# A two-layer transformer block on one core: the order of merging, of the last output projection and of the last tile's mean

## The chip, the core and the metric

The kernel runs on one core of a Trainium2 chip. The metric is the device time of one execution in microseconds. A profile of one execution shows every instruction of the engines: PE (TensorE; PEld is its weight load), DVE (VectorE), ACT (ScalarE), POOL (GpSimd) and SP (SyncE, which issues DMAs).

## What is computed

The input x has 4 x 256 tokens of 512 numbers. Two layers follow, each an attention and a feed-forward step, each added to its input and normalised (mean and variance over the 512 numbers of a token):

```python
x = _layernorm(x + _L0_attn_ref(x, ...))
x = _layernorm(x + _L0_ffn_ref(x, ...))
x = _layernorm(x + _L1_attn_ref(x, w_qkv, w_o))
x = _layernorm(x + _L1_ffn_ref(x, kernel))
```

Layer 1's attention has 8 groups (kv = 0 to 7) of 4 heads of 128 numbers, which share keys and values, with a distance bias and a causal mask. Its output projection is `out @ w_o`, summed over all 8 groups. Its feed-forward step multiplies with a matrix whose 512 rows repeat one block of 64 rows 8 times. All arithmetic is in fp32.

## The kernel before, in words

The tokens stand in 8 tiles of 128 tokens (tt = 0 to 7), two for each batch entry b. `x2[tt]` holds a tile's sum on its way through layer 1. Layer 1's attention is a loop over 64 steps (kv, b, qt), each of 128 queries of 4 heads. `begin1` (L964) makes the scores on PE, adds the bias and takes the maxima on DVE, and makes exponentials and their sums on ACT; `divided` (L282) takes the reciprocals of the sums on DVE (L283) and multiplies the probabilities by them on POOL (L286). `transpose1`, one step later, transposes the probabilities: for kv below 7 by 32x32 blocks on DVE (L312) and DMAs, for kv = 7 on PE (L301). `end1`, one step later again, multiplies with the values on PE (L1012).

For kv below 7, the output projection of both tiles of one b is done with seven products instead of eight (a Strassen scheme in Winograd's form). `outputs1` (L917) first makes four left sums on POOL (`left_sums`, L616 to L621, tile `so`, one buffer); `output_products` then queues the products on PE (L885): four (`po4`), one and five (`po15`, whose second half has the first left sum as weights), six and seven (`po67`, second and third sum), two and three (`po23`, whose second half has the fourth sum). Their results are added on DVE into `x2` (L947, L952) and into `kept[b]` (L898), which collects partial sums over all kv. When the products of b for kv = 6 have been queued, b is put on `merges`; `merge` (L902) then adds `kept[b]` into `x2[2b]` and `x2[2b+1]` with eight additions of 128 x 256 on POOL (L907). The merges 0 to 2 are called from `outputs1` of the next b or from `end1` of kv = 7, merge 3 from `end1`.

For kv = 7, `output1` (L842) multiplies one tile's attention output with the group's weights (four matmuls, L846) and adds it to `x2[tt]` on DVE (L849): the residual. Then `tail1` (L775) of that tile is put on the list of tails. It is a generator; each `yield` ends a piece. Its first piece adds the halves of `x2` on POOL (`half`, L784), takes mean and variance on DVE (`statistics`, L768, tiles `bn_c` and `mv_c`), four times the mean (`four`, L787), `eps` (L789), and the folded and centred tile `xs` (L791). The second transposes `xs` on PE (`pt_xs`, L796) and copies it on ACT (`xsT`, L105). The third multiplies with the feed-forward block on PE (`pf1`, L801), adds on DVE (`z`, L803), takes statistics again (`bn_d`, `mv_d`), forms the reciprocal root on DVE and POOL (`rs`, L808, L809) and the output: on ACT for tiles 0 to 6 (`shift` L820, `yo` L821), on DVE in two halves for tile 7 (L814), each followed by its DMA.

The order of the instructions on each engine is chosen when the program is built: instructions are handed over in the order in which the Python code calls them, and a scheduler may let an instruction pass others. Two calls bind it. `tc.keep_in_program_order` fixes an instruction's place among its engine's, and `tc.issue_after(x)` hands instructions over no earlier than behind the instruction x. [...] After the 64 steps a loop empties the lists `outputs` and `tails` (L1070).

A step or block is named below as (kv, b, qt) or by its b; "pr" tiles are probabilities.

## Time and profile before

| what | value |
|---|---|
| times of three runs, us | 948.67, 951.85, 1353.63 (median 951.85) |
| time of the profiled execution, us | 951.23 |
| its span, first to last instruction, us | 949.3 |
| mean granted TensorE clock | 0.995 of full speed |
| PE busy share of the span | 96% |
| DVE, POOL, ACT busy share | 66%, 47%, 35% |
| the chain that ended last | PE 70%, DVE 12%, POOL 9%, ACT 5% |
| first output product of kv = 6 / start of the last matmul, us from the span's start | 827.93 / 941.83 |

In the rows of a timeline, the first number is the start in us from the span's start, the second the length; then follow engine, line, operation, what is written and read, and in brackets how long the engine sat idle before it and what ended that. Rows of the same kind that follow each other directly are shown as one, with their number behind the x.

### The profile page before, as it was taken

Reading aid. Unit: us, or ns where it says so; the run is one execution under the profiler, and the core shown is the slowest. Engines: PE = TensorE matmul, PEld = TensorE weight load, DVE = VectorE, ACT = ScalarE, POOL = GpSimd, SP = SyncE. Lnnn points to the kernel's source line nnn. Section 1 sums busy time; section 2 is a strip of 40 time slices with the busy share of each in tenths; the row PEclk is TensorE's granted clock in tenths of the full one; section 3 lists DMA queues with packets and bytes.
Section 4 is the critical chain, followed back from the end, with each engine's and each line's share of the span. In section 5 each row is a group of like instructions: output and inputs, shape, how many; then the busy total and the mean of one; then the engine's idle time right before and its main releaser. Section 6 shows DMA issues by size and latency. Waiting matters only on the chain.

```text
span 949.3 us, 11860 instructions
## 1 busy us (share of the span) xinstructions
PE 906.8 (96%) x3849; PEld 554.4 (58%) x3849; DVE 623.8 (66%) x1269; ACT 333.9 (35%) x1216; POOL 444.7 (47%) x462
## 2 busy tenths in 40 slices
PE   7998999898899999999999999999999999999996
PEld 5755555554444445666666566666666666667652
DVE  3986978879434448555676776666666666666566
ACT  2775675677410003323222222122221121214441
POOL 2554553645356124426434533643553534656732
PEclk9999999999999999999999999999999999999998
DMA  9500000000020103543443443353353333432001
GB/s 246 185 1 1 1 2 1 1 1 1 1 89 22 45 1 89 152 111 115 114 130 79 134 132 100 110 140 88 117 139 95 122 89 105 129 89 70 1 34 55
DMA packets 76419, 74.46 MB, mean 78 GB/s; under 512 B 5957, under 2 KB 52678, under 8 KB 76358
## 3 DMA queue, kind: packets, MB, share of 16 engines
q1 hardware_dynamic: 75014, 72.02, 26.4%
q10 hardware_dynamic: 1344, 1.70, 0.6%
q8 instruction: 30, 0.49, 0.2%
q14 instruction: 31, 0.25, 0.1%
HBM read 49.58 MB, written 24.12 MB: 78 GB/s over the span
## 4 chain that ended last, share of the span: by engine, by line
PE 70%; DVE 12%; POOL 9%; ACT 5%; DMA 2%; issue 1%; ACTq 0%; POOLq 0%; SPq 0%; DVEq 0%
PE p_q L636 19%; PE po L885 14%; PE sc L972 7%; PE o L1012 7%; PE p_k L636 5%; PE p_v L636 5%; ACT pr L278 4%; PE py L442 3%; DVE pr L489 3%; PE pf L459 2%; DVE nm L495 2%; PE py L846 2%; POOL x L907 2%; POOL pr L286 2%; DVE prT L103 1%
## 5 line engine op out<-in xcount | busy, mean ns | idle before, releaser
L286 POOL TENSOR_TENSOR pr<-pr,sums 128x512 f32<-128x512 f32 (+1 forms) x128 | 189.5, 1481 | 232.9 <-DVE sums L283 227.4
L278 ACT ACTIVATE pr<-sc,nm 128x128 f32<-128x128 f32 (+1 forms) x256 | 105.0, 419 | 291.1 <-DVE nm L988 277.1
L278 ACT ACTIVATE pr<-pr,nm 128x128 f32<-128x128 f32 (+1 forms) x256 | 113.2, 444 | 39.3 <-DVE sums L283 30.2
L980 DVE SCALAR_TENSOR_TENSOR sc<-table,sc 128x128 f32<-128x128 f32 (+1 forms) x256 | 86.0, 356 | 34.7 <-PE sc L972 32.4
L972 PEld LDWEIGHTS sc<-kT,qT 128*128 128x128 f32 x512 | 82.3, 191 | 35.1 <-issue 29.7
L972 PE MATMUL sc<-kT,qT 128*128 128x256 f32 (+1 forms) x512 | 95.0, 327 | 0.0
L1012 PE MATMUL o<-prT,v 128*128 128x512 f32 x192 | 92.9, 592 | 0.0
L312 DVE STREAM_TRANSPOSE blocks<-pr 128x512 f32<-128x512 f32 x84 | 57.6, 698 | 45.2 <-POOL pr L286 45.1
L650 DVE TENSOR_TENSOR qT<-p_q,qT 128x512 f32<-128x512 f32 x96 | 64.6, 686 | 33.6 <-PE p_q L636 32.8
L988 DVE TENSOR_REDUCE nm<-sc 128x2 f32<-128x512 f32 (+1 forms) x128 | 70.0, 550 | 1.5
L489 DVE TENSOR_TENSOR pr<-sc,causal 128x512 f32<-128x512 f32 (+1 forms) x64 | 60.5, 945 | 10.2 <-PE sc L486 10.0
L301 PE MATMUL pt<-ident,pr 128*128 128x128 f32 x432 | 59.9, 276 | 7.2 <-DVE prT L103 2.1
L495 DVE TENSOR_REDUCE nm<-pr 128x4 f32<-128x512 f32 (+1 forms) x64 | 60.7, 948 | 1.2
L301 PEld LDWEIGHTS pt<-ident,pr 128*128 128x128 f32 x432 | 48.6, 141 | 21.2 <-issue 10.1
L105 ACT COPY o<-o 128x512 f32<-128x512 f32 x29 | 17.0, 587 | 124.9 <-PE o L1012 124.9
L885 PE MATMUL po<-wo,so 128*128 128x256 f32 x224 | 58.0, 381 | 2.1 <-POOL so L616 2.1
L636 PE MATMUL p_q<-x2T,ws_q 128*128 128x512 f32 x128 | 59.8, 592 | 0.0
L636 PE MATMUL p_q<-xt,ws_q 128*128 128x512 f32 x128 | 57.7, 592 | 0.0
L885 PE MATMUL po<-wo,o 128*128 128x256 f32 x224 | 57.7, 380 | 0.0
L636 PE MATMUL p_q<-x2T,wq 128*128 128x512 f32 x128 | 57.6, 592 | 0.0
L105 ACT COPY prT<-pt 128x512 f32<-128x512 f32 x76 | 42.6, 582 | 39.5 <-PE pt L301 39.5
L885 PE MATMUL po<-to,so 128*128 128x256 f32 x224 | 53.3, 381 | 1.0 <-POOL so L619 1.0
(159 smaller groups left out, 1516.8 us busy)
## 6 DMA issues: line engine op xcount, KB each, us to landing
way<-blocks SPq DMA_DIRECT2D x112, 128.0 KB, 2.5
prT<-way SPq DMA_DIRECT2D x28, 512.0 KB, 3.7
wq<-in_L_attn_w_qkv_dram SPq DMA_DIRECT2D x8, 1024.0 KB, 5.1
wo<-in_L_attn_w_o_dram SPq DMA_DIRECT2D x8, 1024.0 KB, 5.4
way<-blocks SPq DMA_DIRECT2D x112, 64.0 KB, 1.8
prT<-way SPq DMA_DIRECT2D x28, 256.0 KB, 2.6
wk<-in_L_attn_w_qkv_dram SPq DMA_DIRECT2D x4, 512.0 KB, 3.8
wv<-in_L_attn_w_qkv_dram SPq DMA_DIRECT2D x2, 1024.0 KB, 6.2
```

What stands on the lines that cost most here:

```text
L278: nc.scalar.activation(pr[:, i, 0:w], sc, AF.Exp, bias=nm[:, i : i + 1], accum_out=sums[:, i : i + 1])
L286: nc.gpsimd.tensor_tensor(pr[:, :, 0:w], pr[:, :, 0:w], sums.unsqueeze(2).to_broadcast([P, G, w]), ALU.mult)
L301: nc.tensor.transpose(pt[:, i, :], pr[:, i, ts(kt, P)], ident)
L489: nc.vector.tensor_tensor(pr[:, :, 0:w], sc[:, :, 0:w], causal[:, 2 * P - w :].unsqueeze(1).to_broadcast([P, G, w]), ALU.add,)
L495: nc.vector.tensor_reduce(nm, pr[:, :, 0:w], AX.X, ALU.max, negate=True)
L636: nc.tensor.matmul(bank, fixed, moving, start=(c == 0), stop=(c == 1))
L650: add = lambda dst, a, b: nc.vector.tensor_tensor(dst, a, b, ALU.add)
L885: nc.tensor.matmul(bank[:, ts(n, HALF)], left[:, c, :], right[:, c, :], start=(c == 0), stop=(c == 1),)
L972: nc.tensor.matmul(sc[:, m, 0:w], qT[:, 2 * j + m, b * S + qt * P : b * S + (qt + 1) * P], kT[:, b * S : b * S + w], start=True, stop=True,)
L980: nc.vector.scalar_tensor_tensor(sc[:, m, 0:w], table[:, 2 * P - w :], slopes[kv * G + 2 * j + m], sc[:, m, 0:w], ALU.mult, ALU.add,)
L988: nc.vector.tensor_reduce(nm[:, 2 * j : 2 * j + 2], sc[:, :, 0:w], AX.X, ALU.max, negate=True)
L1012: nc.tensor.matmul(o, v1[:, 2 * b + kt, ts(kv, P)], prT[:, kt].rearrange("p j h q -> p h j q"), start=(kt == 0), stop=(kt == qt),)
```

## The change

There are three edits.

`divided` returns its POOL instruction, and `begin1` keeps the newest one. `outputs1` binds a merge to that instruction instead of to the last of its own block's left sums. In the compiled program POOL's list changes in one stretch: merge 0 stands ahead of the left sums of b = 1 instead of behind them, merge 1 ahead of those of b = 2, and merge 2 ahead of the division of (7, 1, 0) and of the left sums of b = 3. In merges 0 and 1 the eight additions also stand in another order.

`output1` of tile 7 yields after its second matmul, and the closing loop calls `outputs` ahead of `tails`. In the compiled program PE's list changes in one place: two of tile 7's four output matmuls stand ahead of `pf1_5` instead of behind it.

For tile 7, the residual is a `tensor_tensor_reduce` on DVE, which also sums its result over the row. It is built as two instructions, the main one and one that writes out the sum; the signal to others hangs on the second. `four` is formed from this sum, `xs` follows, and `mv_c` and `eps` come behind `xs`; in the compiled list `bn_c` still stands ahead of `xs`. The lists of ACT and SP are the same as before.

```diff
-        nc.gpsimd.tensor_tensor(
+        return nc.gpsimd.tensor_tensor(
             pr[:, :, 0:w], pr[:, :, 0:w], sums.unsqueeze(2).to_broadcast([P, G, w]), ALU.mult
         )
...
-    def tail1(tt):
+    def tail1(tt, total=None):
...
-        mv = statistics(x, f"c{tt}")
         four = t1.tile([P, 1], F32, tag="four", name=f"four_{tt}", bufs=4)
-        nc.vector.tensor_scalar(four, mv[:, 0:1], 4.0, None, ALU.mult)
+        xs = t1.tile([P, P], F32, tag="xs", name=f"xs_{tt}")
+        add_up = lambda: nc.vector.scalar_tensor_tensor(
+            xs, half[:, 0:P], four, half[:, P:], ALU.subtract, ALU.add
+        )
+        if total is None:
+            mv = statistics(x, f"c{tt}")
+            nc.vector.tensor_scalar(four, mv[:, 0:1], 4.0, None, ALU.mult)
+        else:
+            nc.vector.tensor_scalar(four, total, 4.0 / D, None, ALU.mult)
+            tc.keep_in_program_order(add_up())
+            mv = statistics(x, f"c{tt}")
         eps = t1.tile([P, 1], F32, tag="eps", name=f"eps_{tt}", bufs=4)
         nc.vector.tensor_scalar(eps, mv[:, 1:2], EPS, EPS, ALU.add, ALU.mult)
-        xs = t1.tile([P, P], F32, tag="xs", name=f"xs_{tt}")
-        nc.vector.scalar_tensor_tensor(
-            xs, half[:, 0:P], four, half[:, P:], ALU.subtract, ALU.add
-        )
+        if total is None:
+            add_up()
         yield True
...
-        nc.vector.tensor_tensor(x2[tt], py, x2[tt], ALU.add)
-        tails.append(tail1(tt))
+            if i == 1 and tt == NTT - 1:
+                yield True
+        total = None
+        if tt == NTT - 1:
+            total = t1.tile([P, 1], F32, name="total", bufs=1)
+            nc.vector.tensor_tensor_reduce(
+                out=x2[tt], in0=py, in1=x2[tt], scale=1.0, scalar=0.0,
+                op0=ALU.add, op1=ALU.add, accum_out=total,
+            )
+        else:
+            nc.vector.tensor_tensor(x2[tt], py, x2[tt], ALU.add)
+        tails.append(tail1(tt, total))
         yield True
...
-            done = left_sums(S, A)
+            left_sums(S, A)
             if merges:
-                with tc.issue_after(done.ins):
+                with tc.issue_after(open1["division"].ins):
                     merge()
...
-        divided(pr, sums, w)
+        open1["division"] = divided(pr, sums, w)
         return pr
...
-    while outputs or tails:
-        advance_all(tails, True)
+    while outputs:
         advance(outputs)
         ending.append(True)
+        advance_all(tails, True)
+    while tails:
         advance_all(tails, True)
```

## The prediction, made before the changed kernel ran

> **What bounds the kernel now.** I read the page first (busy time, chain), then the chain in its last 90 us, then the timelines of POOL and PE there, then all engines in the last 20 us.

> ```profile
> PE 906.8 (96%) x3849; PEld 554.4 (58%) x3849; DVE 623.8 (66%) x1269; ACT 333.9 (35%) x1216; POOL 444.7 (47%) x462
> ```

> PE is busy 96% of the span, so a part of the change is worth what it adds to or takes from PE's gaps, plus what it shortens after PE's last product. The chain from 859 to 893 us runs nearly wholly through POOL: POOL's late results make PE's gaps there. POOL's rows (start, length, idle before and its releaser):

> ```profile
> 839.60 1.90 POOL L286 TENSOR_TENSOR pr<-pr,sums 128x1024 f32<-128x1024 f32 x1 [7.16 <-DVE sums L283]
> 843.78 0.73 POOL L616 TENSOR_TENSOR so<-o 128x256 f32<-128x256 f32 x1 [2.29 <-ACT o L105]
> ...
> 846.64 0.72 POOL L907 TENSOR_TENSOR x<-x,kept 128x256 f32<-128x256 f32 x1
> ...
> 852.38 1.04 POOL L286 TENSOR_TENSOR pr<-pr,sums 128x512 f32<-128x512 f32 x1
> 859.34 1.89 POOL L286 TENSOR_TENSOR pr<-pr,sums 128x1024 f32<-128x1024 f32 x1 [5.92 <-DVE sums L283]
> 861.19 0.72 POOL L616 TENSOR_TENSOR so<-o 128x256 f32<-128x256 f32 x1
> ...
> 864.06 0.72 POOL L907 TENSOR_TENSOR x<-x,kept 128x256 f32<-128x256 f32 x1
> ...
> 869.77 2.90 POOL L286 TENSOR_TENSOR pr<-pr,sums 128x512 f32<-128x512 f32 x2
> 875.14 1.04 POOL L286 TENSOR_TENSOR pr<-pr,sums 128x512 f32<-128x512 f32 x1 [2.48 <-DVE sums L283]
> 876.14 0.73 POOL L616 TENSOR_TENSOR so<-o 128x256 f32<-128x256 f32 x1
> ```

> Each merge is eight additions: 846.64 to 852.38, 5.7 us. A group of left sums is four: 861.19 to 864.06, 2.9; its first ends after 0.72. A division takes 1.85 (wide) or 1.0. PE's rows with waits:

> ```profile
> 861.97 1.13 PE L885 MATMUL po<-wo,so 128*128 128x256 f32 x4
> ...
> 870.87 0.65 PE L301 MATMUL pt<-ident,pr 128*128 128x128 f32 x4 [1.73 <-POOL pr L286]
> 871.36 1.06 PE L972 MATMUL sc<-kT,qT 128*128 128x128 f32 x8
> 872.72 0.88 PE L301 MATMUL pt<-ident,pr 128*128 128x128 f32 x6 [0.30 <-POOL pr L286]
> ...
> 877.96 1.03 PE L885 MATMUL po<-wo,so 128*128 128x256 f32 x4
> ...
> 894.68 0.30 PE L796 MATMUL pt_xs<-ident,xs 128*128 128x128 f32 x1 [0.57 <-DVE xs L791]
> ```

> The reader should see that the row at 861.97 starts 0.06 after the sum it needs (861.91): there is no slack for later sums. The end:

> ```profile
> 933.99 1.12 PE L801 MATMUL pf<-wf,xsT 128*128 128x512 f32 x2 [0.88 <-ACT xsT L105]
> 938.70 0.69 DVE L849 TENSOR_TENSOR x<-py,x 128x512 f32<-128x512 f32 x1 [1.58 <-PE py L846]
> 940.62 0.35 DVE L791 SCALAR_TENSOR_TENSOR xs<-half,four 128x128 f32<-128x128 f32 x1
> 943.00 0.75 DVE L803 SCALAR_TENSOR_TENSOR z<-x,mv_c,pf 128x512 f32<-128x512 f32 x1 [0.22 <-PE pf L801]
> ```

> PE's last gap (pt_xs at 932.83 could have been followed at 932.94) is 1.05 us; from 938.66 on, everything is the last tile's chain.

> [...]the division at 852.38 had its sums at 846.46 and stood 5.9 us behind the merge. [...]ScalarE's accumulator reads take 0.19 to 0.21 and end about 0.1 after their main instruction. [...]the trace has 686 for x<-py,x.

> **Part 1, merging.** The compiled order moves merges 0 and 1 from behind to ahead of the left sums of blocks 1 and 2 of kv 6, and merge 2 to ahead of division (7,1,0) and the left sums of block 3. No addition is added or removed and no DMA moves. What stands behind a merge is thereby 5.7 us later on POOL; I follow it in before's clock.

> Merge 0 can start at 841.5, in POOL's idle 2.3 us (the additions PE needs for it end on DVE by 842.6, before the pieces that read them), ends 847.2; sums 847.2 to 850.1, the first at 847.9; PE loads it as weight at 848.7. It just fits, 0.8 to spare. Division (6,3,0) then starts 850.1, 2.3 early. DVE idled 2.8 for it (transpose at 853.45), so its queue moves up as a whole: block transpose 851.1, copy, score additions 852.3 (scores from PE at 851.6 and 852.5), maxima done 855.7; ACT's four exponentials last 1.0, to 856.7; the kept addition ahead of the reciprocal, behind a product ending 855.96, ends 856.7 too. Reciprocal 856.9, division (6,3,1) at 857.0 instead of 859.34.

> Merge 1 follows: 858.9 to 864.6. Block 2's first sum ends 865.3; PE wants it at 861.97: **a new wait of 3.4 us**, with PE's whole queue behind it: the products of block 2, o of (6,3,0), the scores of (7,0,1) and so their softmax on DVE and ACT. DVE's kept addition of this product stands ahead of the reciprocal of (7,0,0), which is thus 867.2, still ahead of POOL's turn for it (867.5). PE is then ready for (7,0,0)'s transposes at 868.97+3.4 = 872.4, and that division is done at 864.6+2.9+1.0 = 868.5, so before's wait until 870.87 is gone: net +1.5. The scores of (7,0,1) come 3.4 later; their sums are ready at about 872.4, the division lasts 872.5 to 874.35, PE goes on at 874.4 instead of 872.72: +1.7.

> Merge 2: 874.35 to 880.1. Then division (7,1,0) to 881.1 and block 3's first sum at 881.8. PE would want it at 877.96+1.7 = 879.66 and gets it at 881.84: +3.9. From there kept 3 waits on POOL for block 3's product (886.1, DVE until 887.0), division (7,1,1) follows at 887.8 to 889.6, ahead of its transposes on PE (890.49+3.9), then the rest of merge 3 and division (7,2,0) to 895.1. The residual of tile 0 follows PE (890.69+3.9, to 895.3), half ends 896.05, xs 896.9, and PE arrives at 894.11+3.9 = 898.0, so the 0.57 wait goes: **+3.3** into the tails, where PE paces all the rest.

> **Part 2, last output projection.** Two matmuls (four passes, 1.72 us) of tile 7 move ahead of pf1_5 into the 1.05 us gap. Their input oT was copied by 929.33. py of tile 7 ends 937.5 instead of 938.66 (932.94 + 1.72 + pf1_5 0.86 + pt_xs 0.11 + 1.72 = 937.35, and 0.16 to drain). Its price: pf1_5 runs 934.66 to 935.7, 0.6 later, so on DVE z_5 starts 935.7 instead of 935.23 and rs_5, last ahead of the residual and 1.89 after z_5's start, ends 937.6. The residual starts 937.6 instead of 938.70, -1.1. If DVE were slower there, the residual would be late next, not PE.

> **Part 3, mean from the residual.** Main instruction: between 0.69[...] and 1.38 (half rate); accumulator read 0.1 to 0.2 more, ahead of any signal to POOL. I take 0.69 and 0.1. POOL's half starts behind shift_5 at 938.6, ends 939.33; bn_c of 0.68 runs meanwhile; xs starts 939.4 instead of 940.62. From xs, the transpose, ACT's copy and pf1_7 take 2.38 to z_7, as before (940.62 to 943.00): 941.8. DVE's own queue needs as long now: mv_c and eps (0.3) stand behind xs, then z_6 to rs_6 (940.90 to 942.78, 1.9). The cover that before was 0.22 of DVE idleness is used up; any more on DVE would count. z_7 is 1.2 earlier than 943.00, and the rest of the chain (6.3 us to the end, the two DMAs in it) is as before. At half rate the residual's signal is 0.7 later and half with it, so 0.6. **-1.2**, bounds -0.5 and -1.3.

> Sum: +3.3 - 1.2 = +2.1 on the profiled 951.23 (span 949.3, 1.9 around it): **953.3**. The two near runs shown, 948.67 and 951.85 (the median, which the profiled run misses by 0.6), say one number wanders by 3 us, more than this effect; about 2%, 19 us, is what a measurement of this kernel can tell from no change.

> **Rivals.** (a) Merging earlier costs PE nothing: its idle 2.3 us on POOL is used, the three POOL waits of PE (1.73+0.30+0.57) go, and the end gains 1.2: 951.23-3.8 = 947.4. For it: POOL is on the chain. Against: the sum at 861.19 starts immediately behind the division, and now has a merge ahead. It decides only if PE reaches the product at 861.97 over 3.4 us later than I have it. (b) Slower: division (6,3,1) is not earlier. Then block 2's first sum comes at 867.6, PE waits 5.7, reaches (7,0,0)'s transposes 3.8 late, and block 3's sums make it about 6: 951.23+6-1.2 = 956. It decides if DVE's queue (kept addition, exponentials) holds the sums until 859. (c) The end gains nothing: the accumulating instruction takes over 2 us. 951.23+3.3 = 954.5. Slower than 2% would need it to take about 18 us more[...], so I leave it 2 in 100.

> **Chances.** Likeliest 0.62 (own range 951.5 to 954.8, terms' bounds alone), (a) 0.13, (b) 0.12, (c) 0.11, the far tail 0.02. The range of 949.3 to 956.5 leaves out most of (a) and the tail, and takes in (b), (c) and the wander. Faster by over 2% 0.01, within 0.97, slower 0.02.

> **What would show it.** Right: PE's po<-wo,so near 862 waits about 3.4 for POOL's L616, the one near 878 about 2.2; the division at 859.34 starts near 857; PE's wait at 870.87 is gone; pf1_5 has no wait behind it, the residual begins 1.1 nearer to its tile's predecessor, xs 1.8 after it. Wrong: no PE wait on left sums, or an accumulating row over 1.4 us.

## The result, and the profile after

| kernel | median, us | lowest to highest | runs | ratio to before [95% interval] |
|---|---|---|---|---|
| before | 949.93 | 947.29 to 1353.63 | 22 | |
| changed | 954.19 | 951.18 to 958.87 | 22 | 1.0046 [1.0033, 1.0059] |

(The 1353.63 is a disturbed execution and is left out of the comparison.) The change makes the kernel slower by 0.46%, some 4.3 us (3.1 to 5.6 by the interval), less than the 2% that count as a difference here, but beyond the interval. The forecast said +2.1. The profiled execution of the changed kernel took 956.8 us, with a span of 954.9 us and a mean TensorE clock of 0.990 (before: 951.23, 949.3, 0.995). First the busy time, from the page of the changed kernel:

```profile
PE 909.2 (95%) x3849; PEld 555.2 (58%) x3849; DVE 624.7 (65%) x1270; ACT 335.3 (35%) x1216; POOL 444.7 (47%) x462
```

POOL's work is the same 444.7 us: the additions were only moved. PE did the same 3849 matmuls, but was busy 2.4 us longer (909.2 against 906.8). That is a first hint that more than waits was added, since idle time is not counted as busy. PE's timeline around the moved merges:

```profile
865.67 1.13 PE L902 MATMUL po<-wo,so 128*128 128x256 f32 x4 [3.50 <-POOL so L616]
866.64 1.68 PE L1029 MATMUL o<-prT,v 128*128 128x512 f32 x2
868.11 2.97 PE L989 MATMUL sc<-kT,qT 128*128 128x256 f32 x8
...
874.37 0.60 PE L301 MATMUL pt<-ident,pr 128*128 128x128 f32 x4
...
876.50 0.88 PE L301 MATMUL pt<-ident,pr 128*128 128x128 f32 x6 [0.64 <-POOL pr L286]
...
883.89 2.06 PE L902 MATMUL po<-wo,so 128*128 128x256 f32 x4 [1.99 <-POOL so L616]
885.75 1.82 PE L1029 MATMUL o<-prT,v 128*128 128x512 f32 x2
```

Both forecast waits are there, 3.50 us for block 2's first left sum and 1.99 for block 3's, and the wait of 1.73 ahead of (7,0,0)'s transposes is gone. But look at the second column: `o<-prT,v x2` takes 1.68 and 1.82 where it takes 1.02 elsewhere, the scores `x8` 2.97 instead of 1.89, and `po<-wo,so x4` 2.06 instead of 1.03. The same matmuls run at about half speed behind each wait. The view by stretches of time says why; its columns are the stretch, its length, the busy time of PE, PEld, DVE, ACT and POOL, and then the granted TensorE clock:

```profile
862.00:865.60 3.60, 0.17 (x1) 0.00 (x0) 0.35 (x2) 1.20 (x7) 3.44 (x6) 1.00 0.55 115
865.60:867.00 1.40, 1.33 (x5) 1.06 (x6) 0.16 (x1) 0.00 (x0) 1.38 (x3) 0.95 0.82 281
867.00:870.40 3.40, 3.40 (x8) 2.19 (x7) 0.96 (x3) 0.59 (x1) 1.73 (x2) 0.52 0.12 42
870.40:880.00 9.60, 8.96 (x48) 7.14 (x47) 5.96 (x16) 5.00 (x19) 5.37 (x7) 1.00 0.00 0
882.00:883.80 1.80, 0.00 (x0) 0.00 (x0) 0.10 (x1) 1.02 (x4) 1.80 (x4) 1.00 0.00 0
883.80:887.40 3.60, 3.51 (x6) 2.16 (x7) 0.69 (x1) 0.00 (x0) 2.76 (x5) 0.53 0.00 0
```

PE idles, resumes, and for about 3.4 us gets a clock of 0.52 or 0.53; then it is 1.00 again (the row from 870.40; behind 887.40 too). Below, this is called a clock fall; its exact edges stand in the section on after_again1 and after_again2. POOL's order came out as worked out: merge 0 begins at 841.54, block 1's sums at 847.38, division (6,3,0) at 850.24 (forecast: 841.5, 847.2, 850.1). The end, on DVE:

```profile
944.52 0.69 DVE L861 CUSTOM_DVE_ANT_0 x<-py,x 128x512 f32<-128x512 f32 x1
945.14 0.08 DVE L861 DVE_READ_ACCUMULATOR2_ANT total<- 128x1 f32 x1
946.29 0.35 DVE L787 SCALAR_TENSOR_TENSOR xs<-half,four 128x128 f32<-128x128 f32 x1 [0.28 <-POOL half L784]
...
948.67 0.75 DVE L810 SCALAR_TENSOR_TENSOR z<-x,mv_c,pf 128x512 f32<-128x512 f32 x1
```

The accumulating residual takes 0.69 us, as the plain one did; its read 0.08. `xs` starts 1.77 us behind it (before: 1.92).

### One clock for all executions

The times from the span's start are not comparable between executions: the division (6,2,1), which stands at 839.60 in the profile of before and ahead of everything that the change moves, starts at 835.29 to 840.11 in the fourteen profiles of this study, although every instruction up to it is in the same order. So this table counts from that division. Rows are named by the experiments below. "First sum" and "fourth sum" are PE's products with these left sums. The end of the span is taken to the hundredth, where the pages round it to a tenth.

| execution | division at | block 2, first sum | block 2, fourth sum | block 3, first sum | pt_xs of tile 0 | residual of tile 7 | its z | end of span | length of last pf1 |
|---|---|---|---|---|---|---|---|---|---|
| before | 839.60 | 22.37 | 28.51 | 38.36 | 55.08 | 99.10 | 103.40 | 109.66 | 1.13 |
| changed | 839.69 | 25.98 | 33.81 | 44.20 | 61.98 | 104.83 | 108.98 | 115.24 | 1.12 |
| after_again1 | 837.75 | 25.95 | 33.78 | 44.15 | 60.24 | 103.08 | 107.22 | 113.49 | 1.13 |
| after_again2 | 840.11 | 25.94 | 33.77 | 44.14 | 60.23 | 103.07 | 107.21 | 113.47 | 1.13 |
| merge_only | 839.73 | 25.97 | 33.74 | 44.13 | 60.21 | 104.21 | 109.06 | 115.33 | 1.67 |
| ends_only | 837.32 | 22.35 | 28.49 | 38.36 | 55.07 | 97.94 | 102.32 | 108.58 | 1.35 |
| projection_only | 837.21 | 22.35 | 28.49 | 38.34 | 55.06 | 97.94 | 103.16 | 109.44 | 2.05 |
| mean_only | 837.53 | 22.35 | 28.49 | 38.35 | 55.06 | 99.08 | 103.00 | 109.27 | 1.12 |
| first_merge_ends | 839.09 | 22.31 | 28.35 | 37.34 | 54.07 | 96.94 | 101.19 | 107.46 | 1.24 |
| two_merges_ends | 837.15 | 25.97 | 33.80 | 42.03 | 58.63 | 101.50 | 106.10 | 112.37 | 1.58 |
| split_second_merge | 837.99 | 22.31 | 28.35 | 36.57 | 53.46 | 96.34 | 100.47 | 106.74 | 1.13 |
| fill_second | 837.45 | 25.97 | 33.81 | 44.20 | 60.28 | 103.13 | 107.27 | 113.55 | 1.13 |
| fill_first_wait | 835.29 | 26.01 | 32.15 | 41.52 | 59.34 | 102.19 | 106.33 | 112.59 | 1.13 |
| fill_first_again | 839.39 | 25.96 | 32.10 | 41.46 | 62.30 | 105.13 | 109.32 | 115.59 | 1.18 |

Up to pt_xs of tile 0 the rows with the same POOL order agree within 0.1 us, except where a clock fall stands between. That makes differences of 0.3 us readable in a single profile that the medians, with intervals of 1.2 us to each side and more, can't give.

### The profile page after: what moved, and what is told of

It is laid out like the page before. It is cut to its first block, busy times and chain, and to the rows that moved or that the text cites. A ratio compares the mean times of both kernels' runs of the same rounds, so it can differ in the third digit from the quotient of the medians.

```text
span 954.9 us, 11860 instructions
## 1 busy us (share of the span) xinstructions
PE 909.2 (95%) x3849; PEld 555.2 (58%) x3849; DVE 624.7 (65%) x1270; ACT 335.3 (35%) x1216; POOL 444.7 (47%) x462
## 4 chain that ended last, share of the span: by engine, by line
PE 73%; DVE 12%; POOL 8%; ACT 5%; issue 1%; DMA 1%; ACTq 0%; POOLq 0%; DVEq 0%
PE p_q L636 19%; PE po L902 15%; PE sc L989 8%; PE o L1029 8%; PE p_k L636 5%; PE p_v L636 5%; ACT pr L278 4%; PE py L442 3%; DVE pr L489 3%; PE pf L459 2%; PE py L853 2%; DVE nm L495 2%; POOL pr L286 2%; PE pq L403 1%; DVE prT L103 1%; POOL x L924 1%
## 5 line engine op out<-in xcount | busy, mean ns | idle before, releaser
L286 POOL TENSOR_TENSOR pr<-pr,sums 128x512 f32<-128x512 f32 (+1 forms) x128 | 189.5, 1481 | 235.1 <-DVE sums L283 224.0
L997 DVE SCALAR_TENSOR_TENSOR sc<-table,sc 128x128 f32<-128x128 f32 (+1 forms) x256 | 86.2, 356 | 37.0 <-PE sc L989 34.7
L301 PE MATMUL pt<-ident,pr 128*128 128x128 f32 x432 | 59.8, 276 | 5.9 <-DVE prT L103 2.1
L105 ACT COPY o<-o 128x512 f32<-128x512 f32 x29 | 17.0, 587 | 132.0 <-PE o L1029 132.0
L301 PEld LDWEIGHTS pt<-ident,pr 128*128 128x128 f32 x432 | 48.6, 141 | 19.6 <-issue 10.2
L105 ACT COPY prT<-pt 128x512 f32<-128x512 f32 x76 | 42.7, 582 | 39.9 <-PE pt L301 39.9
```

The costliest lines, as they stand in the source:

```text
L286: return nc.gpsimd.tensor_tensor(pr[:, :, 0:w], pr[:, :, 0:w], sums.unsqueeze(2).to_broadcast([P, G, w]), ALU.mult)
L301: nc.tensor.transpose(pt[:, i, :], pr[:, i, ts(kt, P)], ident)
L997: nc.vector.scalar_tensor_tensor(sc[:, m, 0:w], table[:, 2 * P - w :], slopes[kv * G + 2 * j + m], sc[:, m, 0:w], ALU.mult, ALU.add,)
```

## The experiments

The theory after this first profile: merging earlier makes two waits on PE, each costs its idle time less the waits that it replaces, and on top of that up to 1.9 us for a clock fall behind it (an estimate: the longer rows above add 1.74 us behind the first wait and 1.83 behind the second). The rivals: the whole loss is idle time on POOL's account, and the long rows belong to the order of instructions; or the end does not gain what was said.

### merge_only and ends_only: the parts alone

The first edit alone (`divided` returns its instruction, `outputs1` binds the merge to it), and the second and third alone (`outputs1` as before).

> Only the merges are moved (part 1); the end is as before. My theory (the loss is PE's two waits for left sums, about 3.4 and 2.0 us, and a halved TensorE clock for some us behind each of them in about half of the executions): PE reaches the first transpose of a tail (pt_xs of tile 0) 3.3 us late without and up to 7 us late with the lower clock, the median is 5 to 6 us above before, ratio 1.005 to 1.007. Rival (the loss lies in the two edits at the end, the accumulating residual above all): ratio 1.000, no late PE at pt_xs.

Measured: 956.45 us median (953.52 to 960.42, 6 runs), ratio 1.0082 [1.0057, 1.0106].

> Only the two edits at the end (parts 2 and 3); the merges stand as before. My theory: 1.3 us shorter than before, ratio 0.9986; z of the last tile starts 1.3 us earlier than 943.0, and no wait of PE for left sums is longer than before's. Rival (the end edits lose): ratio 1.002 or more, z of the last tile later than 943.

Measured: 948.03 us (946.47 to 951.22, 22 runs), ratio 0.9987 [0.9974, 1.0001].

The loss is merging's, the end gains. In the table, merging delays pt_xs of tile 0 by 60.21 - 55.08 = 5.1 us with one clock fall (behind the first wait; the second wait, 2.00 us, had none). The end's edits shorten the end by 109.66 - 108.58 = 1.08 us, and by 0.22 more if the last product had its old length (last column: 1.35 against 1.13). Their median's interval holds 1.000, so the timed runs alone do not show that gain; the anchored trace does, step by step.

### projection_only and mean_only: the end taken apart

On the kernel before, only the second edit:

```diff
+            if i == 1 and tt == NTT - 1:
+                yield True
...
-    while outputs or tails:
-        advance_all(tails, True)
+    while outputs:
         advance(outputs)
         ending.append(True)
+        advance_all(tails, True)
+    while tails:
         advance_all(tails, True)
```

> Before with the second edit alone: two of tile 7's four output products ahead of pf1_5. If the step of the prediction holds (residual 1.1 us earlier), 1.1 us less than before, 948.8, ratio 0.9988, and in the trace the residual starts about 5.8 us behind the start of pf1_4's product, where before had 4.71 + 1.1; that is, the row of the residual follows py directly and pf1_5 has no wait. Rival, that DVE's queue eats it (rs_5 late ahead of the residual): ratio 1.000, and DVE without idle time ahead of the residual.

Measured: 949.40 us (945.83 to 951.80, 14 runs), ratio 0.9997 [0.9984, 1.0011]. The residual comes 99.10 - 97.94 = 1.16 us earlier, as said, but the span ends only 0.22 earlier. DVE is not the reason: it waits 1.15 us for the last product. PE's row of that product, and the clock around it, in projection_only:

```profile
937.58 0.30 PE L796 MATMUL pt_xs<-ident,xs 128*128 128x128 f32 x1 [1.61 <-DVE xs L791]
938.28 2.05 PE L801 MATMUL pf<-wf,xsT 128*128 128x512 f32 x2 [0.41 <-ACT xsT L105]
```
```profile
938.20:940.40 2.20, 2.05 (x2) 0.48 (x2) 0.98 (x4) 0.11 (x2) 0.82 (x2) 0.53 0.19 70
```

Another clock fall, behind waits of 1.61 and 0.41 us with one transpose between. It cost 2.05 - 1.13 = 0.92 us, and 0.22 + 0.92 is 1.14, the gain of the residual. The last column of the table shows this at the end of five executions, in sizes from 0.11 (first_merge_ends) to 0.92, whatever the edit; in the others it is below 0.1.

The third edit alone:

> Before with the third edit alone: tile 7's residual also sums, xs from this sum. From the changed kernel's trace (xs 1.77 us behind the residual's start against 1.92, accumulator read 0.08): 0.1 to 0.2 us less than before, ratio 0.9998, z_7 4.15 us behind the residual's start against 4.30. Rival, that this edit is what gives the end its gain: 1 us less, ratio 0.999, z_7 under 3.5 us behind the residual's start.

Measured: 949.84 us (946.82 to 952.11, 14 runs), ratio 0.9999 [0.9984, 1.0013]; in the trace the end comes 0.39 us earlier, `xs` stands 1.55 us behind the residual, `z` 3.92. That is more than expected. The expectation was taken from the changed kernel, where `xs` waits 0.28 us for POOL: there `half` stands behind `shift_5`. POOL's rows in mean_only and then in ends_only:

```profile
935.75 0.27 POOL L827 TENSOR_SCALAR shift<-mv_d,rs 128x1 f32<-128x1 f32 x1
937.39 0.73 POOL L784 TENSOR_TENSOR half<-x 128x256 f32<-128x256 f32 x1 [1.38 <-DVE total L859]
```
```profile
936.05 0.27 POOL L827 TENSOR_SCALAR shift<-mv_d,rs 128x1 f32<-128x1 f32 x1
936.28 0.72 POOL L784 TENSOR_TENSOR half<-x 128x256 f32<-128x256 f32 x1
```

With the residual at its old time POOL is idle and takes `half` at once; with it 1.16 us earlier, POOL is still at the tail ahead. So the two edits share a part of their gain: 1.16 for the projection, 0.4 for the mean alone, and about 0.14 for the mean on top of it (`xs` 1.78 behind the residual in ends_only, against 1.92 in before).

### first_merge_ends and two_merges_ends: merges one by one

Both have the end's edits; merge 0 alone, or merges 0 and 1, follow the newest division, the others stay behind their block's sums:

```diff
-            left_sums(S, A)
+            done = left_sums(S, A)
             if merges:
-                with tc.issue_after(open1["division"].ins):
+                with tc.issue_after((open1["division"] if b == 1 else done).ins):
```

(two_merges_ends has `b < 3`.)

> The edits at the end, and of the merges only merge 0 bound to the newest division; merges 1 and 2 behind their left sums as before. My theory: merge 0 fits into POOL's idle 2.3 us without making PE wait, the division of (6,3,1) and all behind it on POOL come 1.1 to 2.3 us earlier, PE's wait of 1.73 for the transposes of (7,0,0) shrinks to about 0.6: 2.4 us below before, ratio 0.9975. Rival (any merge ahead of left sums costs PE time): not below the version with the end edits alone, ratio 0.9986 or more.

Measured: 946.68 us (944.47 to 950.62, 22 runs), ratio 0.9967 [0.9955, 0.9980].

> The changed kernel with only merges 0 and 1 behind the newest division; merge 2 stays behind the left sums of block 3. POOL's order alone differs. PE's first wait (3.5 us for block 2's first sum) stays, the second (2.0 us, block 3's) should be gone. Theory that each wait costs its idle time less what it replaces, plus up to 1.9 us for the lower TensorE clock that follows it: about 5 us of the change's rise over first_merge_ends fall to the two waits in the ratio 3 to 4, so 950 to 951.5, ratio 1.000 to 1.0017, with the rows behind the first wait (po with so as weights, sc, o) showing 1.3 to 1.8 instead of 1.03 in the executions with the clock fall. Rival, that the first wait is the whole loss: 953 or more, 1.0035 and up. Rival, that the second is: as first_merge_ends, 0.9967.

Measured: 951.71 us (949.54 to 956.34, 22 runs), ratio 1.0018 [1.0005, 1.0030], just above the 950 to 951.5 expected.

From the first to the second, pt_xs of tile 0 goes from 54.07 to 58.63: merge 1 costs 4.56 us, of which 1.69 is the clock fall behind its wait (the way from first to fourth sum is 7.83 us in two_merges_ends, 6.14 in before). From there to the changed kernel, merge 2 costs 1.6 us without a fall (60.24) and 3.35 with one (61.98). Merge 0 gains about 1 us, in POOL's idle 2.3. Both rivals on record fall: neither wait is the whole loss.

### fill_first_wait, fill_first_again, fill_second: PE kept at work during a wait

The changed kernel, with matmuls ahead of the waiting product whose results are overwritten by it; seven ahead of block 2's (both fill_first), four ahead of block 3's (fill_second). The diff shows the first of the two; fill_second has `{3: 4}`:

```diff
+        fill = {2: 7}.get(b, 0) if kv == NKV - 2 else 0
...
-            bank = products(f"po15_{name}", [(A[0, 0], Bm[0, 0]), (S1, T1)])
+            bank = products(f"po15_{name}", [(A[0, 0], Bm[0, 0]), (S1, T1)], fill)
...
+            for _ in range(fill * n):
+                nc.tensor.matmul(
+                    bank[:, ts(n, HALF)], pairs[0][0][:, 0, :], pairs[0][1][:, 0, :],
+                    start=True, stop=True,
+                )
```

> The changed kernel with 7 more matmuls on PE (128x128 by 128x256, about 3.0 us in all) ahead of the product that waits for block 2's first left sum; their results are overwritten, so the output is that of the kernel. They fill most of the 3.5 us wait; some instructions further on change places. My theory (the clock falls because PE stands idle): the clock stays 1.00 behind this place, the scores of (7,0,1) take 1.9 us instead of 2.97, and the products six and seven of block 2 start at about 869.1 instead of 870.9. Rival (the clock falls for another reason[...]): the scores still take about 3 us in half or more of the executions, and six and seven start at 870.9 or later.

Measured: 954.57 us (950.06 to 956.10, 9 runs), ratio 1.0044 [1.0024, 1.0064].

> Another look at the version whose first wait is filled with seven overwritten matmuls, unaltered. In six of six executions with that wait unfilled the rows behind it were long (block 2's second pair of products with sums starts 7.8 us behind the waiting product). Theory that PE's idle time lowers the clock: 6.14 us again, as in the first look and in the kernel before. Rival, that the first look was an accident: 7.8.

Measured: 956.95 us in one run (a run of before beside it took 949.43), span 955.0. The filled wait in fill_first_again, and the wait that this kernel has for block 3's sum, not filled:

```profile
865.35 1.13 PE L910 MATMUL po<-wo,so 128*128 128x256 f32 x4 [0.46 <-POOL so L616]
866.32 1.02 PE L1039 MATMUL o<-prT,v 128*128 128x512 f32 x2
867.17 1.89 PE L999 MATMUL sc<-kT,qT 128*128 128x256 f32 x8
...
880.85 2.08 PE L910 MATMUL po<-wo,so 128*128 128x256 f32 x4 [3.51 <-POOL so L616]
...
884.43 1.92 PE L1039 MATMUL o<-prT,v 128*128 128x512 f32 x2
```

and the same second wait in fill_first_wait, the same program in another execution:

```profile
876.81 1.13 PE L910 MATMUL po<-wo,so 128*128 128x256 f32 x4 [3.51 <-POOL so L616]
...
878.65 1.02 PE L1039 MATMUL o<-prT,v 128*128 128x512 f32 x2
```

The sum arrives just as late (26.0 in the table), but with PE at work until 0.5 us before it, the rows behind it are 1.13, 1.02 and 1.89 in both executions, and the fourth sum follows 6.14 us later as in before. Unfilled, it was 7.77 to 7.84 in six executions of six. So PE's idle time brings the fall, not the late sum. The two executions also show that the fall is not a matter of order: behind the same wait of 3.51 us, one has rows of 2.08 and 1.92, the other 1.13 and 1.02, and pt_xs of tile 0 comes at 62.30 and 59.34, 2.96 us apart. The version saves nothing in the median: the filling made the scheduler set later instructions in another order, with the second wait 3.51 us instead of 1.99.

> The changed kernel with four more matmuls of 128x256 (1.7 us) ahead of block 3's waiting product on PE, whose results are overwritten; all other orders are the same. Theory of the clock: PE's idle time ahead of block 3's product falls from 2.0 to about 0.3 us, the rows behind it keep 1.03 (po) and 1.02 (pt, sc), and the executions that showed the fall are up to 1.9 us shorter: median 952.5 to 954, ratio 1.003 to 1.004. Rival, that only the idle time counts and the clock does not: 954.2 as the changed kernel, 1.0046, with the rows behind the filled wait as long as in the changed kernel (2.06 and 1.82).

Measured: 953.02 us (952.59 to 956.41, 9 runs), ratio 1.0039 [1.0021, 1.0057]. Its wait was 0.27 us, its rows behind had no fall, pt_xs of tile 0 came at 60.28. This fits, but tells nothing apart: three other executions with the wait unfilled (merge_only and the two below) had no fall there either, and the median's interval holds the changed kernel's.

### after_again1 and after_again2: the changed kernel, profiled again

> Another look at the changed kernel, unaltered, for how often the TensorE clock falls behind each of the two waits. Counted from the start of the division that stands at 839.69 in its first profile: the waiting product of block 2 starts at 25.98 in every execution, the transposes of (7,0,0) at 34.7 with a clock fall and 33.0 without; block 3's product at 44.2 or 42.5; tile 0's pt_xs at 61.98 with both falls, 60.2 with one. Rival, that these delays belong to the order of instructions and not to the clock: the same 34.68 and 61.98 again, with rows of the same lengths.

> A further look at the changed kernel, unaltered; expected as in the look before it: 61.98 us from the division to tile 0's pt_xs with two clock falls, 60.2 with one, 58.5 with none; the rival says 61.98 always.

Measured: 953.33 and 955.68 us, spans 951.2 and 953.6. The rows in after_again1 behind the two waits:

```profile
863.70 1.73 PE L902 MATMUL po<-wo,so 128*128 128x256 f32 x4 [3.48 <-POOL so L616]
865.23 1.91 PE L1029 MATMUL o<-prT,v 128*128 128x512 f32 x2
866.93 2.18 PE L989 MATMUL sc<-kT,qT 128*128 128x256 f32 x8
...
881.90 1.13 PE L902 MATMUL po<-wo,so 128*128 128x256 f32 x4 [1.98 <-POOL so L616]
882.87 1.02 PE L1029 MATMUL o<-prT,v 128*128 128x512 f32 x2
```

One fall each, pt_xs of tile 0 at 60.24 and 60.23 as the theory says for one, where the rival had 61.98. The fall behind the first wait begins at another place than in the first profile (there `po` was still 1.13 and the scores 2.97), but costs the same 1.69 us. From the division to the end, the changed kernel is thus 113.49 - 109.66 = 3.83 us slower with one fall and 5.58 with two; the measured +4.3 lies between.

What decides whether a wait brings a fall can be read from the edges of the falls. In each of the fourteen profiles, the times at which the granted clock changes lie whole multiples of 3.413 us apart, to within 0.001 us. Where this grid lies against the program differs from execution to execution: its first edge behind the division above comes 1.8 to 3.3 us after that division's start. So the traces can be cut into windows of 3.413 us. The rows give PE's busy time and its granted clock in such windows, in the changed kernel and then in before, fill_first_wait and fill_first_again (the columns are the stretch, its length, PE's busy time and the clock, then two of DMA):

```profile
863.46:866.87 3.41, 1.20 (x5) 1.00 0.47 129
866.87:870.28 3.41, 3.41 (x8) 0.50 0.15 55
880.52:883.94 3.42, 1.43 (x8) 1.00 0.00 0
883.94:887.35 3.41, 3.41 (x6) 0.50 0.00 0
```
```profile
869.00:872.41 3.41, 1.68 (x13) 1.00 0.41 150
872.41:875.83 3.42, 3.12 (x16) 1.00 0.00 0
```
```profile
871.66:875.07 3.41, 1.63 (x8) 1.00 0.00 0
875.07:878.48 3.41, 1.67 (x11) 1.00 0.00 0
878.48:881.90 3.42, 3.42 (x18) 1.00 0.00 0
```
```profile
876.76:880.17 3.41, 0.58 (x3) 1.00 0.00 0
880.17:883.58 3.41, 2.73 (x9) 0.50 0.00 0
883.58:887.00 3.42, 3.42 (x10) 0.50 0.00 0
```

This accounts for the single cases. In fill_first_wait an edge splits the wait of 3.51 us into halves, both windows stay at 48 and 49%, and the clock holds. In fill_first_again nearly the whole wait lies in one window (17%), and the window at half clock behind it, itself only 80% busy, is followed by a second one. That is why the same wait cost 2.96 us more there. The wait of about 2 us brought a fall where it lay in one window whole, as in the first profile (42%); in the two later ones and in merge_only an edge divided it. Before's wait of 1.73 us lies in one window whole and still leaves it 49% busy. That idle time is the cause, the fill has shown; the border itself is read from the traces, and no experiment was made to set it.

### split_second_merge: is there more in the order that won?

first_merge_ends, with the second half of merge 1 (four additions) moved behind division (7,0,1):

```diff
         add(top[:, HALF:], U)
+        if split:
+            return lambda: rest(add, low, U, M5, M7)
+        rest(add, low, U, M5, M7)
...
+                    open1["rest"] = merge(b == 2)
...
         open1["division"] = divided(pr, sums, w)
+        if (kv, b, qt) == (NKV - 1, 0, 1):
+            with tc.issue_after(open1["division"].ins):
+                open1["rest"]()
```

> As the version with the end's edits and only merge 0 behind the newest division, but merge 1 in two halves: four additions behind block 2's left sums, the other four behind division (7,0,1). POOL's order alone differs. That division is then not behind the whole merge: the divisions of (7,0,0) and (7,0,1) start about 2.8 us nearer to their sums, PE's two waits of 0.88 and 0.30 us for them go. 1.2 us less than that version's 946.7, so 945.5, ratio 0.9955 to before, 0.9945 to 0.997 with the interval. Rival, that the second half is late for division (7,1,0) and block 3's sums instead: 946.7, with a new wait on POOL's L616 behind 875 us.

Measured: 947.13 us (944.39 to 951.59, 22 runs), ratio 0.9972 [0.9959, 0.9984]. In the trace it gains 0.6 us to pt_xs of tile 0 (53.46 against 54.07), not 1.2: the wait of 0.88 for (7,0,0) is gone, but the one for (7,0,1) grew from 0.30 to 0.63, its division now waiting 2.07 us for its own sums instead of for POOL. The medians do not tell it from first_merge_ends. Both beat the kernel before; which of them is better stays open.

## Why the prediction was right or wrong

The direction was right, and the measured 954.19 us lies in the stated range; but one term was left out. That it lies even within the forecast's narrower range of 951.5 to 954.8 is luck in part: no bound of that range held a price for the clock.

**Merging, POOL's side: right.** The merge fits in the idle 2.3 us, and division (6,3,1) starts at 857.21 (forecast 857.0). Rival (a), that it costs nothing, would have needed PE to come late; it came at once and waited 3.50 us (3.4). Rival (b) had this division not earlier. Its 956 us is near the profiled 956.8, but for a wrong reason: no wait of 5.7 us is in any profile.

**Merging, PE's side: the step that failed.** The forecast carried the waits along PE's queue with the row lengths of before: +1.5 at (7,0,0)'s transposes, +1.7 at (7,0,1)'s, +3.9 at block 3's sum, "**+3.3** into the tails". Measured at block 3's sum: 44.20 - 38.36 = +5.84, less 1.69 for the fall +4.15. Measured at pt_xs of tile 0: +6.90, less 1.69 and 1.74 for the two falls +3.47; in the two later profiles, with one fall, +5.16, less 1.69 again +3.47. So the waits were sized within 0.3 us, and the term left out was the clock behind them: 1.7 us for each fall (half of the 3.413 us at half clock), one or two in each of the three profiles. An execution of the changed kernel without any was not seen; the +3.47 is worked out. What was measured directly is that a filled wait leaves the rows at their old length.

The page of before could not show the price as a row: its own PE wait of 1.73 us at 870.87 kept the clock at 1.00, here as in ends_only, projection_only and mean_only. But its trace held a clock fall further ahead, in layer 0, behind waits of 1.02 and 0.73 us with one group of matmuls between (the columns are those of the first view by stretches):

```profile
53.21:56.63 3.42, 1.68 (x13) 0.80 (x11) 3.38 (x5) 3.36 (x13) 2.65 (x2) 1.00 0.00 0
56.63:60.04 3.41, 3.41 (x5) 1.35 (x4) 1.49 (x3) 3.04 (x13) 2.85 (x2) 0.50 0.02 5
```

PE was busy for 49% of the first stretch, and in the second its clock was 0.50. The new wait of 3.4 us stood in the forecast's own text, nearly twice the idle time of that stretch (1.74 us), and should have been checked against this. Nor need a window be idle as a whole: behind the division, PE busy for 46% of it or less was enough, so a wait of 1.99 us sufficed once in four, and one of 3.51 us, split by an edge, once did not.

**The end: right.** The residual of tile 7 comes 1.16 us earlier (1.1), `xs` 1.77 behind it (1.8), and the accumulating instruction costs what the lower bound said (0.69, read 0.08; the upper bound of 1.38 was an estimate, twice the plain row's 0.69). That it is two instructions on DVE is now to be seen in its two rows at L861. From pt_xs of tile 0 to the end the changed kernel gains 6.90 - 5.58 = 1.32 us (1.34 in after_again1), against 1.2. Rival (c), that the end gains nothing, falls.

**The sum.** +3.47 and -1.32 give +2.15, the forecast; with one fall it is +3.83, with two +5.58, measured from a division that stands ahead of all that was changed. The three profiles hold four falls; an estimate from these, 2.15 + 4/3 x 1.7 = 4.4, meets the median's +4.3, though three profiles are few.

## What to carry to other kernels

When a change puts a wait of some 2 us or more on PE, where it is otherwise busy without a gap (here one of 1.98 to 2.00 us brought a clock fall in one execution of four), look at the granted clock behind it and price the work that follows at half speed as one bound: here a wait of 3.5 us cost 1.7 us more than its length in most executions, 3.0 in one and nothing in one. Compare traces from a common instruction just ahead of the change instead of from the span's start, and a single profile settles tenths of a microsecond where the medians wander by whole ones. The work moved earlier on POOL's queue was free only as far as the queue's idle 2.3 us reached: the first merge gained 1 us, the next two cost 4.6 and 1.6 to 3.4.

## What the runs showed of the hardware that was not expected

- A wait on PE of 3.46 to 3.51 us brought a clock of half speed in seven executions of eight, one of 1.98 to 2.00 in one of four, one of about 1.7 in none of four, and filled waits of 0.27 to 0.51 in none of three. The windows of 3.413 us decide the single case. An estimate from the border of 46% that the windows behind the division show: in an otherwise full stretch, a wait must leave 54% of one window, 1.8 us, idle. By it a shorter one would bring no fall, one of twice that length would bring one wherever the edge lies, and between them the edge decides.
- In all fourteen profiles the clock also falls at the kernel's end, behind waits of 1.2 to 1.6 and 0.41 us. Whether the last two matmuls lie ahead of that edge or behind it made them last between 1.12 and 2.05 us.
- The first 840 us, the same instructions in the same order, took 835.3 to 840.1 us to the same division. This spread is as large as the effect studied, and it goes with the clock too. At the start of before, one matmul of `pq` follows the other by 0.43 us until the clock is first recorded as full, at 15.7 us, and by 0.22 after that. With full clock from 9.8 to 11.5 us on, the division came at 835.3 in the one execution with no fall ahead of it, at 837.1 to 838.0 in the seven with one, and at 839.1 to 839.7 in the three with two. In the other three the clock was full only from 15.7 to 16.3 us on, and with one fall the division came at 839.6 to 840.1.
